# Two-layer graph network on one Trainium2 core: layer one's first score stage moved behind the plain block, weight and token sums dealt out by a kept clock per engine, token sums in a lent tile place

## Chip, cores and metric

The kernel runs on one core of one Trainium2 chip. The metric is the device time in microseconds (us) of that core, as the median of several runs. The kernel before takes 2650.01 us (three runs, 2649.26 to 2651.77).

## What is computed

The input x has 128 graphs of 64 nodes with 768 features, and adj is a 0/1 matrix of 64 by 64 for each graph. First h = relu(layernorm(x)). Then two layers follow, with weights of 768 by 768 each:

```python
m_left  = h @ W_left[l].T ;  m_right = h @ W_right[l].T
u_left  = h @ m_left^T / sqrt(768) ;  u_right = h @ m_right^T / sqrt(768)
u   = u_left on and above the diagonal of adj, u_right below it
att = exp(u)*adj / (row sum of exp(u)*adj + 1e-10)
ctx = att @ (h @ W_lin[l].T + b_lin[l])
h   = relu(layernorm(ctx, std with ddof=1, eps 1e-3) * a + b)
```

The result is x + h. Everything is in 32-bit floats. The weights are handed in transposed, and adj comes with its transpose beside it.

## The kernel before, in words

The 8192 tokens are cut into 32 parts of 256 tokens. A part's h lies transposed (features on the partitions) in an `ht` tile of six 128 x 256 chunks; six such tile places exist. The parts are grouped in blocks: block 0 has parts 0 and 1, blocks 1 to 10 have three parts each.

Each layer has two passes (the four calls stand at L1332 to L1335). **Pass one** makes M, the products of h with W_left and W_right combined, then the scores (L733, small matmuls of M with h), and from them the attention of a block (a chain of steps on POOL, DVE and ACT, `chain`, L737 to L779), which is stored to DRAM. **Pass two** multiplies with W_lin and applies the attention (L1006 and further).

In pass one a block of three parts is not multiplied plainly. A fast matrix multiplication scheme is used with 40 **products** (`PRODUCTS`, numbered 0 to 39). A product multiplies one sum of weight blocks, called a form (v = 18 to 118), with one sum of token blocks (T9 to T46), in eight matmuls of 128 x 256 at L702. Its result in a PSUM bank is read (L910 by ACT if it is the first into that part of M, L245 and L914 by DVE otherwise) and added into M. There are four banks in turn in a chain of products (C, D, X, Y, then C again), so product i+4 needs the reads of product i to be over.

- **Token sums** (`Tokens`, L583 to L638): 38 operations per block, on POOL, at L245, from `ht` chunks or earlier sums. `step` (L610) emits the next if the block's tokens are ready, if fewer than 11 (`LIMIT`) sums are out and if a buffer is free; `need` (L635) emits all that are missing right before the product that wants them. A token sum's buffer is a 128 x 512 place `g` of a common first-in-first-out list `free`; it goes back to the list when its last product is issued.
- **Weight sums** (`Weights`, L478 to L546): 101 operations, for layer one made on the chip while it runs, on DVE and POOL. `some` (L531) emits the first operation within reach whose operands exist. During the plain block an operand is first copied into a spare PSUM bank by ACT (L517; banks Z, V and the score bank in turn, `stage`), so that DVE reads only one operand from SBUF. For layer two the forms are made in pass two of layer one (`sums_ahead`, L549) and loaded from DRAM.

**What sets the order.** TensorE's program is written as a chain of products. Everything else is handed out in `turn_of` (L832), which is called twice for each product: once in its middle and once after it. Each call is a *slot*; product i of a block covers the slots 2i and 2i+1 after the block's first slot. `turn_of` runs what a plan has for that slot (`put`, `put_all`), then lets weight sums and one token sum follow as a small planner clock allows: `clock["vector"]` and `clock["pool"]` are compared with `now`, the estimated time of the slot. In the kernel before, this `clock` is a fresh local of each pass one (L830), starting at 0. Each engine carries out its own instructions in the order in which they were handed out.

**Layer one's block 0** is the *plain block*: 12 groups of 24 matmuls (L877 to L891), 72 slots, with no scheme, since the weight sums do not exist yet. Block 1 of layer one then begins with the scheme; in the kernel before the scores of block 0 come after its product 3 (`SCORED`, L925), the reads of products 0 to 3 behind the scores, and the attention chain at slot 2*SCORED+4 of block 1. Rows of x for the next parts are loaded, normalised (`mean_var` L333, L397 to L412), transposed (L465) and stored as h beside this (`prepare`, L850).

**The last block of pass one** (block 10) also gets `final` (L1310 to L1326): the W_lin blocks are loaded and centred on ACT (L233, L237), and from them come the sums N0 to N16 for pass two: Nn is planned at slot 42 + 3n//2 of the block, even n on POOL and odd n on DVE. The token sums for pass two's first parts (ta, u1, u2, u0, u3, td and more, on POOL) are planned at slots 56, 58 and so on.

Of the kernel before, what the change touches and what calls it, by code (L numbers as in the profile page):

```python
# [10 lines left out]
F32 = mybir.dt.float32  # L11
# [6 lines left out]
def kernel(  # L18
# [57 lines left out]

    def timed(us, f):
        f.vector = us
        return f

    def run(slot):
# [304 lines left out]
    def transpose_rows(l, u, pool):  # L386

        key, xr, todo = (1, l, u), XR[l, u], []
        if l == 0:
            mv = stat.tile([P, Q, 2], F32, name="mv0", bufs=2)  # L390
            sd = stat.tile([P, Q], F32, name="sd0", bufs=2)
            rs = stat.tile([P, Q], F32, name="rs0", bufs=2)
            nb = stat.tile([P, Q], F32, name="nb0", bufs=2)

            def scale(q0, q1):
                def deviation():
                    nc.scalar.activation(sd[:, q0:q1], mv[:, q0:q1, 1], AF.Sqrt, bias=eps_in)  # L397
# [16 lines left out]
            stats = [timed(1.2, lambda q=q: mean_var(mv[:, q, :], [xr[q][:, :HH], xr[q][:, HH:]])) for q in range(Q)]  # L414
            norms = [lambda q=q: norm(q) for q in range(Q)]
            if u:
                for f in stats + [lambda: [f() for f in scale(0, Q)]] + norms:
                    todo.extend([f, None])
            else:

                dev, inv = zip(*(scale(q, q + 1) for q in range(Q)))
                todo.extend([stats[START[0]], dev[START[0]]])
                for q, after in zip(START, START[1:] + (None,)):
                    if after is not None:
                        todo.append(stats[after])
                    todo.append(inv[q])
                    if after is not None:
                        todo.append(dev[after])
                    if q == START[2]:

                        todo.append(lambda: turn(0, START[0]))
                    todo.append(norms[q])
# [31 lines left out]
        for q in range(Q):  # L464
            todo.append(timed(0.9, lambda q=q: nc.vector.transpose(  # L465
                xb[:, :, q, :], xr[q].rearrange("p (b j) -> p b j", j=32))))
            todo.append(None)
# [3 lines left out]
    def places(pool, shapes, names):  # L471
        for n in names:
            shape, bufs = shapes[n]
            pool.tile(shape, F32, name=n, bufs=bufs)

    class Weights:  # L478
        def __init__(self, ops, plain, stay, extra=()):
# [10 lines left out]
            self.mine = {id(t) for t in extra}  # L490
            self.extra = deque(extra)

        def used(self, v):
# [5 lines left out]
        def take(self):  # L499
            of = max(self.extra, free, key=len)  # L500
            return of.popleft() if of else None

        def emit(self, eng, op):
            v, a, ca, b, cb = op
            x, y = self.at[a], self.at[b]
            dead = next((s for s in (a, b) if self.uses[s] == 1 and not (self.mine and s >= 18)), None)
            t = self.take() if dead is None else self.at[dead]
            if t is None:
                return False
            if dead is not None:  # L510
                self.uses[dead] = 0
                del self.at[dead]
            if self.stage and eng is nc.vector:
                bank = self.stage.pop(0)
                self.stage.append(bank)
                bank = bank.rearrange("p (c d) -> p c d", c=K2)
                nc.scalar.copy(bank, x)  # L517
                x = bank
            if ca == 1:
# [10 lines left out]

        def some(self, eng, reach=10):  # L531
            for op in self.left[:reach]:
                if op[1] in self.at and op[3] in self.at and (eng is nc.vector or op[2] == 1):
                    if eng is nc.vector and op[2] == 1 and any(o[2] != 1 and o[1] in self.at and o[3] in self.at
                                                               for o in self.left[:reach // 2]):
                        continue
                    return self.emit(eng, op)
            return False

        def need(self, v):  # L540
            if v not in self.at:
                op = next(o for o in self.left if o[0] == v)
                self.need(op[1])
                self.need(op[3])
                assert self.emit(nc.vector, op)
            return self.at[v]  # L546

# [35 lines left out]
    class Tokens:  # L583
        LIMIT = 11

        def __init__(self, l):
# [5 lines left out]
            self.count = {}  # L592


        def value(self, k, v, cut=False):
# [14 lines left out]
        def step(self, slot, eng=None):  # L610
            if self.k >= len(SUPER) or slot < self.ready.get(self.k, 10 ** 9) or self.out >= self.LIMIT or not free:
                return False
# [26 lines left out]


    SPACE = (((0, 46, 97), (-12, 34, 97)), ((10, 46, 97), (10, 46, 97)))

# [12 lines left out]
    def pass_one(l, start, final):  # L655
        with tc.tile_pool(name=f"one{l}", bufs=2, reuse_waits="tile") as sp, \
# [172 lines left out]
            weights.at = W[l, "raw"]  # L829
            clock = {"pool": 0.0, "vector": 0.0}  # L830

            def turn_of(slot):  # L832
                now = slot * 0.86 if l == 0 or slot >= 80 else slot * 0.6 + 20.8
                clock["vector"] = max(clock["vector"], now - 1.0) + sum(getattr(f, "vector", 0.0) for f in plan.get(slot, ()))
# [12 lines left out]

            follow = {}

            def prepare(b, slot, step=1):  # L850
# [5 lines left out]
                for t in range(2):  # L856
# [5 lines left out]
                    if before >= 0:  # L862
                        at = max(at, begins(where[before][0] + 1, l) + 2 * SCORED + 3)
                    put(at, lambda p=p, hold=before >= 0: load_part(1, l, p, hold))
                    put_all(at + lag + 6 * t, affine_part(1, l, p))
# [13 lines left out]
            for n, (w, t) in enumerate(order):  # L879
                bank = bank_of(n % CHAINS)  # L880
                for j in range(3):
                    tok = HT[1, l, t][:, j * K2:(j + 1) * K2, :]
                    product(bank, weights.at[3 * w + j], [tok], j == 0, slot)
                    weights.used(3 * w + j)
                    if j == 2:
                        if n == 0 and mid:
                            mid()
                            weights.stage = [KEEP["Z"], KEEP["V"], KEEP["scores"][:, 0]]
                        nc.scalar.copy(into(6 * t + w), out_of(bank))
                    turn_of(slot + 1)  # L890
                    slot += 2  # L891
            weights.stage = []

            last = len(SUPER) - 1
            for k in range(FIRST_OF[l], len(SUPER)):
                assert slot == begins(k, l)
                if k:
                    put_all(slot + 2 * SCORED + 4, softmax(k - 1), 3)
                    put(slot + 2 * SCORED + 42, lambda k=k: load_adj(k, nc.scalar))
# [4 lines left out]
                def reads(i):  # L904
                    for o, c in READS[i]:
                        bank = out_of(bank_of(CHAINS * (k - 1) + i % CHAINS), k == 0, o)
                        to = into(o, k == 0)
                        if o not in seen:
                            seen.add(o)
# [6 lines left out]
                for i, (f, t) in enumerate(PRODUCTS):  # L916
# [448 lines left out]
```

## Time and profile before

| what | value |
|---|---|
| median of three runs | 2650.01 us (2649.26 to 2651.77) |
| the profiled execution | 2648.42 us, its span 2646.6 us |
| granted TensorE clock, mean | 0.995 |
| DVE busy | 1780.6 us (67%), 2888 instructions |
| ACT busy | 935.4 us (35%), 1969 instructions |
| POOL busy | 1763.1 us (67%), 1392 instructions |

All rows below are from that one profiled execution. Times count from the start of its span. A row of the timeline gives start, length, engine, source line, operation, result and operands, shape and the number of instructions of the same kind in a row (x24), and in brackets the idle time of the engine ahead of it and the instruction that ended it. Engines: PE is TensorE, DVE is VectorE, ACT is ScalarE, POOL is GpSimd, SP is the queue that issues DMAs.

### The profile page before, as it was taken

Reading aid. Unit: us, or ns where it says so; the run is one execution under the profiler, and the core shown is the slowest. Engines: PE = TensorE matmul, PEld = TensorE weight load, DVE = VectorE, ACT = ScalarE, POOL = GpSimd, SP = SyncE. Lnnn points to the kernel's source line nnn. Section 1 sums busy time; section 2 is a strip of 40 time slices with the busy share of each in tenths; the row PEclk is TensorE's granted clock in tenths of the full one; section 3 lists DMA queues with packets and bytes.
Section 4 is the critical chain, followed back from the end, with each engine's and each line's share of the span. In section 5 each row is a group of like instructions: output and inputs, shape, how many; then the busy total and the mean of one; then the engine's idle time right before and its main releaser. Section 6 shows DMA issues by size and latency. Waiting matters only on the chain. (4 is left out here: it accounts for less than half of the span.)

```text
span 2646.6 us, 47202 instructions
## 1 busy us (share of the span) xinstructions
PE 2591.6 (98%) x18122; PEld 2217.1 (84%) x18122; DVE 1780.6 (67%) x2888; ACT 935.4 (35%) x1969; POOL 1763.1 (67%) x1392
## 2 busy tenths in 40 slices
PE   9899999999999999999999999999999989999998
PEld 8788888888888888888798888888888878887886
DVE  7878787777768445554456667677666676666667
ACT  5522223223113244454542222122222335555453
POOL 4766676666668657676276666667666657878786
PEclk9999999999999999999999999999999999999999
DMA  7443534343421354445794424253532215555655
GB/s 220 113 111 86 124 93 110 93 119 79 98 60 56 123 156 149 159 139 182 219 282 101 121 68 108 71 129 93 136 98 70 67 49 157 157 167 166 177 161 146
DMA packets 258465, 331.84 MB, mean 125 GB/s; under 512 B 56002, under 2 KB 190402, under 8 KB 258242
## 3 DMA queue, kind: packets, MB, share of 16 engines
q1 hardware_dynamic: 241442, 320.56, 44.3%
q10 hardware_dynamic: 16800, 8.26, 1.2%
q8 instruction: 145, 2.38, 0.4%
q14 instruction: 78, 0.64, 0.1%
HBM read 213.39 MB, written 115.34 MB: 124 GB/s over the span
## 5 line engine op out<-in xcount | busy, mean ns | idle before, releaser
L245 POOL TENSOR_TENSOR g<-ht 128x512 f32<-128x512 f32 (+1 forms) x620 | 785.9, 1279 | 420.8 <-PE Z L702 71.6
L245 POOL TENSOR_TENSOR g<-g,g 128x512 f32<-128x512 f32 (+1 forms) x310 | 397.9, 1291 | 136.7 <-PE C L702 22.0
L245 POOL TENSOR_TENSOR g<-ht,g 128x512 f32<-128x512 f32 (+1 forms) x272 | 346.1, 1282 | 164.8 <-PE Z L702 42.8
L702 PE MATMUL X<-g,g 128*128 128x256 f32 (+1 forms) x1080 | 252.9, 377 | 6.0 <-DVE m L914 6.0
L1006 PE MATMUL Z<-g,g 128*128 128x256 f32 x1024 | 244.1, 380 | 3.5 <-ACT hl L300 3.2
L702 PE MATMUL C<-g,g 128*128 128x256 f32 x1008 | 239.7, 381 | 4.9 <-POOL g L245 2.2
L702 PEld LDWEIGHTS X<-g,g 128*128 128x128 f32 x1080 | 203.0, 191 | 34.8 <-DVE m L914 6.8
L702 PE MATMUL Y<-g,g 128*128 128x256 f32 (+1 forms) x968 | 225.7, 376 | 3.8 <-POOL g L245 3.8
L1006 PEld LDWEIGHTS Z<-g,g 128*128 128x128 f32 x1024 | 191.6, 190 | 35.8 <-issue 4.1
L379 ACT ACTIVATE ht<-ht,b_col,a_col 128x256 f32<-128x256 f32 x384 | 196.1, 591 | 69.0 <-DMA ht<-h 53.8
L702 PEld LDWEIGHTS C<-g,g 128*128 128x128 f32 x1008 | 190.5, 190 | 32.9 <-POOL g L245 3.5
L702 PE MATMUL Z<-g,g 128*128 128x256 f32 (+1 forms) x936 | 217.0, 375 | 0.0
L702 PE MATMUL D<-g,g 128*128 128x256 f32 x880 | 209.8, 381 | 1.8 <-POOL g L245 1.8
L702 PEld LDWEIGHTS Y<-g,g 128*128 128x128 f32 x968 | 182.0, 190 | 27.8 <-POOL g L245 4.2
L702 PE MATMUL V<-g,g 128*128 128x256 f32 (+1 forms) x840 | 194.6, 375 | 3.1 <-POOL g L245 1.6
L702 PEld LDWEIGHTS Z<-g,g 128*128 128x128 f32 x936 | 174.5, 190 | 23.1
L702 PEld LDWEIGHTS D<-g,g 128*128 128x128 f32 x880 | 168.1, 191 | 25.7 <-POOL g L245 2.5
L1006 PE MATMUL X<-g,g 128*128 128x256 f32 x768 | 182.7, 379 | 0.0
L702 PEld LDWEIGHTS V<-g,g 128*128 128x128 f32 x840 | 157.6, 191 | 23.3 <-POOL g L245 1.7
L1206 POOL TENSOR_TENSOR z<-z,b 128x768 f32<-128x768 f32 x62 | 112.7, 1829 | 81.7 <-DVE z L1203 77.2
L245 DVE TENSOR_TENSOR m<-m,Y 128x512 f32<-128x512 f32 (+2 forms) x196 | 126.5, 667 | 58.4 <-ACT m L910 35.7
L245 DVE TENSOR_TENSOR m<-m,D 128x512 f32<-128x512 f32 x180 | 118.2, 677 | 70.0 <-ACT m L910 51.3
(222 smaller groups left out, 4612.0 us busy)
## 6 DMA issues: line engine op xcount, KB each, us to landing
ht<-h SPq DMA_DIRECT2D x126, 768.0 KB, 6.3
h<-xb SPq DMA_DIRECT2D x124, 384.0 KB, 6.6
z<-z SPq DMA_DIRECT2D x128, 192.0 KB, 3.1
x<-z SPq DMA_DIRECT2D x128, 192.0 KB, 5.4
xr<-in_x_dram SPq DMA_DIRECT2D x120, 192.0 KB, 3.8
out_dram<-xr SPq DMA_DIRECT2D x120, 192.0 KB, 2.7
x<-in_x_dram SPq DMA_DIRECT2D x112, 192.0 KB, 5.4
g<-form SPq DMA_DIRECT2D x40, 256.0 KB, 5.6
```

Source lines behind the costliest of these rows:

```text
L245: (eng.tensor_add if sign == "+" else eng.tensor_sub)(o, a, b)
L379: nc.scalar.activation(ht, ht, AF.Relu, bias=cols[1][:, c:c + 1], scale=cols[0][:, c:c + 1])
L702: nc.tensor.matmul(o, w[:, c, g * P:(g + 1) * P], t, start=(new and g == c == at == 0), stop=(c == K2 - 1), skip_group_check=True)
L1006: nc.tensor.matmul(p[:, n], b[t][:, c, r * P:(r + 1) * P], w[s][:, c, :], start=(i in FIRST and i not in PRELOAD and n == c == 0), stop=(c ...
L1206: nc.gpsimd.tensor_add(zs[k], zs[k], rows["b"])
```

## The change

1. **The scores of block 0** are issued right behind the plain block, ahead of product 0 of block 1. Its attention chain is planned from slot 2 of block 1, and the reads of block 1's products follow each product at once.
2. **The planner's clock** is made once for the whole kernel, with an entry for each of DVE, ACT and POOL. It is set at the start of layer one's pass one only (`if not l`). Each weight sum gets an estimated start (`begins`) from when its operands, its buffer, its engine and its stage bank are free; `some` takes the one that can start first and none that would start over 3 us ahead. Weight sums that are still missing at the end of the plain block are staged through banks Z and V in block 1.
3. **The lent place.** The `ht` tile place of part 5 is taken early, and its three 128 x 512 thirds serve as buffers for token sums of block 1 that are last used before product 20 (`SOON`). The load of part 5 itself moves to slot 113 (`back`), behind those of parts 6 and 7 in the SP queue.
4. The row statistics of parts 2 to 5 start at slots 19 and 31 instead of 16 and 30, and POOL may take weight sums from slot 0 instead of slot 8. Set beside each other in order, the two programs have the same instructions on TensorE; the new one has 11 fewer on DVE, 6 fewer on ACT and 10 more on POOL, as more of the weight sums go to POOL ahead of slot 60. Twenty of the weight sums are now emitted behind the plain block, between the products 0 and 20 of block 1; before, three were.

The core of the diff:

```diff
+    clock = {"vector": 0.0, "scalar": 0.0, "pool": 0.0}
...
     def load_part(which, l, p, hold=False):
-        ht = HT[which, l, p] = big.tile([P, C, TH], F32, name="ht", bufs=6)
+        if (which, l, p) not in HT:
+            HT[which, l, p] = big.tile([P, C, TH], F32, name="ht", bufs=6)
+        ht = HT[which, l, p]
...
+        def begins(self, eng, op):
+            dead = self.dead(op)
+            t = self.at[dead] if dead is not None else (self.extra or free or (None,))[0]
+            x, y = (self.made.get(s, 0) for s in (op[1], op[3]))
+            at = max(y, self.until.get(id(t), 0), clock[NAMES[eng]])
+            if self.stage and eng is nc.vector:
+                x = max(x, clock["scalar"], self.until.get(id(self.stage[0]), 0)) + 0.6
+            return max(x, at)
...
+        def some(self, eng, reach, now):
...
+            at, _, op = min(ops)
+            return at <= now + 3 and self.emit(eng, op)
...
         def emit(self, eng):
             v, a, b, sign = self.queue.pop(0)
-            t = free.popleft()
+            t = (self.own if self.own and self.last[v] < SOON else free).popleft()
...
             if v >= 9 and n == self.uses[v]:
-                free.append(self.at.pop((k, v)))
+                t = self.at.pop((k, v))
+                (self.own if id(t) in self.mine else free).append(t)
...
-            clock = {"pool": 0.0, "vector": 0.0}
+            if not l:
+                clock.update(vector=3.0, scalar=0.0, pool=3.0)
...
             def turn_of(slot):
-                now = slot * 0.86 if l == 0 or slot >= 80 else slot * 0.6 + 20.8
+                now = slot * 0.87 if l == 0 or slot >= 80 else slot * 0.6 + 20.8
...
+                for e in clock:
+                    clock[e] = max(clock[e], now - 0.5)
...
                 if weights.left and slot >= start["weights"]:
-                    while clock["vector"] <= now and weights.some(nc.vector):
-                        clock["vector"] += 0.62
-                    if clock["pool"] <= now and start["pool"] <= slot < start["tokens"]:
-                        if weights.some(nc.gpsimd, 40):
-                            clock["pool"] = max(clock["pool"], now) + 1.35
+                    while clock["vector"] <= now + (2 if slot > 2 * PLAIN else 0.5) and weights.some(nc.vector, 10, now):
+                        pass
+                    if slot < start["tokens"]:
+                        while clock["pool"] <= now + 0.5 and weights.some(nc.gpsimd, 40, now):
+                            pass
+                tokens.limit = Tokens.LIMIT - 2 * bool(weights.left)
                 if clock["pool"] <= now + 1.5 and tokens.step(slot):
                     clock["pool"] = max(clock["pool"], now) + 1.35
+            if l == 0:
+                for p in range(2, 6):
+                    HT[1, 0, p] = big.tile([P, C, TH], F32, name="ht", bufs=6)
+                tokens.own.extend(HT[1, 0, 5][:, j * K2:(j + 1) * K2, :] for j in range(3))
+                tokens.mine = {id(t) for t in tokens.own}
+
+                def back():
+                    assert len(tokens.own) == 3
+                    tokens.own.clear()
+                    load_part(1, 0, 5)
+
+                put(begins(1) + 2 * SOON + 1, back)
...
-            weights.stage = []
+            weights.stage = [] if l else [KEEP["Z"], KEEP["V"]]
+            if not l:
+                scores(0)
...
-                    put_all(slot + 2 * SCORED + 4, softmax(k - 1), 3)
+                    put_all(slot + (2 * SCORED + 4 if l or k > 1 else 2), softmax(k - 1), 3)
...
-                    if i == SCORED and k:
+                    if i == SCORED and l + k > 1:
                         scores(k - 1)
-                    if i >= SCORED or k == 0:
+                    if i >= SCORED or l + k < 2:
...
-    pass_one(0, {"weights": 0, "pool": 8, "tokens": 60, 1: 16, 2: 30}, final_of(0))
+    pass_one(0, {"weights": 0, "tokens": 60, 1: 19, 2: 31}, final_of(0))
```

More of the change, by code (lines that the diff above doesn't have):

```diff
@@ L474, in places @@
             pool.tile(shape, F32, name=n, bufs=bufs)
+    NAMES = {nc.vector: "vector", nc.gpsimd: "pool"}
     class Weights:
@@ L505, in emit @@
             x, y = self.at[a], self.at[b]
-            dead = next((s for s in (a, b) if self.uses[s] == 1 and not (self.mine and s >= 18)), None)
+            dead, at = self.dead(op), self.begins(eng, op)
+            if dead is None and len(free) <= self.spare:
+                return False
             t = self.take() if dead is None else self.at[dead]
@@ L529, in emit @@
             return True
[L531 to L538, printed above, removed]
+        def some(self, eng, reach, now):
+            ops = [(max(self.begins(eng, op), now) + (0.4 if eng is nc.vector and op[2] == 1 else 0), n, op)
+                   for n, op in enumerate(self.left[:reach])
+                   if op[1] in self.at and op[3] in self.at and (eng is nc.vector or op[2] == 1)
+                   and (len(free) > self.spare or self.dead(op) is not None)]
+            if not ops:
+                return False
+            at, _, op = min(ops)
+            return at <= now + 3 and self.emit(eng, op)
         def need(self, v):
@@ L592, in __init__ @@
             self.count = {}
+            first = {t: i for i, (_, t) in reversed(list(enumerate(PRODUCTS)))}
+            for v, a, b, _ in reversed(T_OPS):
+                for s in (a, b):
+                    first[s] = min(first.get(s, 99), first[v])
+            self.last = {v: max([i for i, (_, t) in enumerate(PRODUCTS) if t == v] +
+                                [first[o] for o, *ab, _ in T_OPS if v in ab]) for v, *_ in T_OPS}
+            self.own, self.mine, self.limit = deque(), set(), self.LIMIT
         def value(self, k, v, cut=False):
@@ L610, in step @@
         def step(self, slot, eng=None):
-            if self.k >= len(SUPER) or slot < self.ready.get(self.k, 10 ** 9) or self.out >= self.LIMIT or not free:
+            if self.k >= len(SUPER) or slot < self.ready.get(self.k, 10 ** 9) or self.out >= self.limit or not free:
                 return False
```

64 lines of the change are left out of this document (49 added, 15 removed).

## The prediction

> **What bounds the kernel now.** I read the page first, then the waits and the timeline of TensorE over layer one's start, then the same engine and POOL in the last block of each pass one. The page:
>
> ```profile
> span 2646.6 us, 47202 instructions
> PE 2591.6 (98%) x18122; PEld 2217.1 (84%) x18122; DVE 1780.6 (67%) x2888; ACT 935.4 (35%) x1969; POOL 1763.1 (67%) x1392
> ```
>
> TensorE is busy for 2591.6 of 2646.6 us, so at most 55 us are idle, and its own work is the same in the new program. What the change can do is to fill holes of TensorE or to open new ones. The timeline of TensorE at the hole in question, and a window over it:
>
> ```profile
> 69.55 5.34 PE L702 MATMUL Y<-ht,g 128*128 128x256 f32 x24
> 77.08 2.51 PE L702 MATMUL C<-g,g 128*128 128x256 f32 x8 [2.19 <-POOL g L245]
> 81.39 3.78 PE L702 MATMUL D<-g,g 128*128 128x256 f32 x8 [1.79 <-POOL g L245]
> 84.96 2.03 PE L702 MATMUL X<-g,g 128*128 128x256 f32 x8
> 90.80 2.57 PE L702 MATMUL Y<-g,g 128*128 128x256 f32 x8 [3.80 <-POOL g L245]
> 93.30 5.16 PE L733 MATMUL sc<-m,ht 128*32 128x95 f32 x192
> 99.49 1.97 PE L702 MATMUL C<-g,g 128*128 128x256 f32 x8 [1.04 <-ACT m L910]
> 101.30 1.89 PE L702 MATMUL D<-g,g 128*128 128x256 f32 x8
> ...
> 106.48 1.89 PE L702 MATMUL C<-g,g 128*128 128x256 f32 x8
> ...
> 128.92 1.89 PE L702 MATMUL D<-g,g 128*128 128x256 f32 x8
> ```
> ```profile
> 74.89:99.49 24.60, 15.78 (x225) 12.52 (x225) 20.55 (x35) 14.57 (x27) 18.94 (x16) 0.79 0.50 127
> 99.49:128.92 29.43, 29.43 (x136) 25.83 (x137) 23.68 (x44) 12.74 (x21) 21.27 (x18) 1.00 0.30 66
> ```
>
> The last plain group ends at 69.55 + 5.34 = 74.89. The four rows of 8 matmuls up to 90.80 are products 0 to 3 of block 1, then come the scores (L733), and 99.49 is product 4; 128.92 is product 21. Between 74.89 and 99.49 TensorE is busy for 15.78 of 24.60 us at a granted clock of 0.79 (the columns of a window are length, then busy time of PE, PEld, DVE, ACT, POOL, then the clock). From product 4 on it runs without a gap: (128.92 - 99.49) / 17 = 1.73 us per product. All three waits name POOL at L245, the token sums; these in turn wait for buffers that DVE's late weight sums hold:
>
> ```profile
> 83.09 2.51 POOL L245 TENSOR_TENSOR g<-ht 128x512 f32<-128x512 f32 x2 [1.75 <-DVE g L522]
> 88.13 2.61 POOL L245 TENSOR_TENSOR g<-ht,g 128x512 f32<-128x512 f32 x2 [2.53 <-DVE g L522]
> ...
> 108.51 1.28 POOL L245 TENSOR_TENSOR g<-g,g 128x512 f32<-128x512 f32 x1 [0.52 <-PE C L702]
> ```
>
> **Step 1: the hole in layer one (gain).** The change puts the scores where the first waits were, and they need no token sum. Another block's scores of the same size show the full-clock price:
>
> ```profile
> 1399.42 4.13 PE L733 MATMUL sc<-m,ht 128*32 128x95 f32 x192
> ```
>
> I let them start at 74.75 (as a product follows 0.16 us before the modelled end of the one before it) and take 4.13 plus 0.5 for the last copies of M by ACT: product 0 at 79.4, and without any wait product 4 at 79.4 + 4 x 1.73 = 86.3 instead of 99.49. That is **13.2 us** at best. Three things take some of it back.
>
> (a) *POOL.* In the order of the new program T16 goes to a third of the lent place that is freed by product 1, and product 3 wants it. Product 1 ends at 79.4 + 1.73 + 1.89 = 83.0; POOL started 0.14 us after such an end (106.48 + 1.89 = 108.37, row at 108.51), so T16 starts near 83.15, and POOL's queue is in order: T16 to T23 are eight sums of 1.27 (2.51 / 2 in the row at 83.09), ready at 83.15 + 10.2 = 93.3. Product 7 wants T23 and would start at 79.4 + 7 x 1.73 = 91.5. Cost 1.8, and 0.3 more for the same at products 9 and 11: **2.1 us**.
>
> (b) *DVE.* Twenty weight sums now lie between products 0 and 20. One staged sum, one statistics step, one mask step and one transpose:
>
> ```profile
> 89.10 0.68 DVE L245 TENSOR_TENSOR g<-sc,g 128x512 f32<-128x512 f32 x1
> 89.70 1.59 DVE L245 TENSOR_TENSOR g<-g,g 128x512 f32<-128x512 f32 x1
> 91.21 1.01 DVE L336 BATCH_NORM_STATS2 st<-x 128x6 f32<-128x384 f32 x2
> 92.25 0.21 DVE L337 BATCH_NORM_AGGREGATE mv<-st 128x2 f32<-128x12 f32 x1
> ```
>
> Staged sums follow each other at 0.60 (89.70 - 89.10), so 20 cost 12.0. The window 99.49:128.92 shows 23.7 us of DVE work beside products 4 to 20 (their reads, the attention chain, transposes); three of the four row statistics at 1.2 lay ahead of it and now come along, 3.7. Sum 39.4 us against 21 x 1.73 = 36.3 for products 0 to 20: 3.1 too much, part of which may trail behind product 20 in the four banks. The bounds are 0 and 3.1 plus a late start; by the order of the reads against the banks I take **2.1 us**. ACT's 20 copies of some 0.6 have cover (12.74 busy of 29.43).
>
> (c) *One buffer.* T37 now takes the place that T36 leaves after product 20, and product 21 wants it: 0.16 (overlap lost) + 0.14 + 1.27 + the start of the matmuls, **1.7 us**; 0 if that place is not the last one. The row 81.39 shows a price beyond: after a gap of 1.79 the eight matmuls took 3.78 in place of 1.89, while after the gap of 1.04 at 99.49 they took 1.97. My 1.7 lies between; I take no slow clock here and keep 1.9 us for the range. [...]
>
> Step 1: 13.2 - 2.1 - 2.1 - 1.7 = **7.3 us gained**, with 3 and 11 as ends (all three twice as dear; only (a) left). The load of part 5, and SP's queue with it, I cost at nothing:
>
> ```profile
> ht<-h SPq DMA_DIRECT2D x126, 768.0 KB, 6.3
> ```
>
> Part 5 opens block 2 at slot 152, 39 slots or 34 us behind slot 113; such a load lands in 6.3 us, and the stores of attention that now stand ahead of it in SP's queue are wanted by pass two only. If that cover were gone, block 2's first token sums and so its first product would wait for what is missing.
>
> **Step 2: layer two (loss).** The clock is set for layer one alone. At the end of layer one's pass one `clock["pool"]` stands near 870 x 0.87 = 757, and in layer two `now` starts at 20.8. The condition `clock["pool"] <= now + 1.5` then fails up to slot (757 - 1.5) / 0.87 = 868 of 880. So no token sum of layer two's blocks is given out ahead: each is emitted by `need`, right before its product. In blocks 0 to 9 that hardly matters: POOL's queue is in order and mostly waits for buffers that TensorE frees, and a sum emitted late in the program still starts when its buffer is free. The rows of POOL and TensorE from 1500 to 2060:
>
> ```profile
> L245 POOL TENSOR_TENSOR g<-ht 128x512 f32<-128x512 f32 x134 | 169.8, 1275 | 100.2 <-PE X L702 33.3 <-PE Z L702 30.1 <-PE C L702 27.7
> PE sc L733 <- issue: 2.8, 5, 0.9
> ```
>
> The first shows the waits for TensorE, the second that TensorE waited for no sum there. I take 0 for these blocks; the other end is a rival below. In the last block POOL also carries the even N sums, and these wait for ACT and DVE. Before, the token sums were handed out ahead of most of them; now T39 (wanted by product 23) stands behind N2, T41 (product 25) behind N4 and T44 (product 32, slot 64) behind all that is planned up to slot 63: N8, ta, N10, u1, N12, u2, u0, N14. TensorE and POOL there, before:
>
> ```profile
> 2121.62 1.89 PE L702 MATMUL Y<-g,g 128*128 128x256 f32 x8
> ...
> 2125.07 1.89 PE L702 MATMUL D<-g,g 128*128 128x256 f32 x8
> ...
> 2137.22 3.38 PE L702 MATMUL X<-g,g 128*128 128x256 f32 x8 [3.10 <-DVE m L914]
> ...
> 2142.17 1.89 PE L702 MATMUL C<-g,g 128*128 128x256 f32 x8
> ```
> ```profile
> 2121.96 1.27 POOL L245 TENSOR_TENSOR g<-g,g 128x512 f32<-128x512 f32 x1 [3.37 <-ACT g L968]
> ...
> 2127.81 1.27 POOL L245 TENSOR_TENSOR g<-g,g 128x512 f32<-128x512 f32 x1 [2.11 <-ACT g L237]
> ...
> 2139.64 1.28 POOL L245 TENSOR_TENSOR g<-g,g 128x512 f32<-128x512 f32 x1 [1.94 <-DVE g L245]
> 2140.88 1.73 POOL L245 TENSOR_TENSOR g<-ht 128x512 f32<-128x512 f32 x1
> ...
> 2146.70 1.72 POOL L245 TENSOR_TENSOR g<-g,g 128x512 f32<-128x512 f32 x1
> ```
>
> The products are 23, 25, 30 and 32; the sums are N2, N4, N10, u1 and N14. N2 starts at 2121.96 whatever is ahead, so T39 ends at 2121.96 + 2 x 1.27 = 2124.5: product 23 is 2.9 late. N4 starts at 2127.81, then T41 ends at 2130.4: product 25 is 5.3 late. Product 30 waited 3.10 for DVE before; that wait now lies inside the delay, and product 30 comes at 2130.4 + 5 x 1.73 = 2139.0, 1.8 late. N10 waits for DVE's N9, which stands behind the reads around product 30: 2139.64 + 1.8 = 2141.4. From N10's start to N14's end POOL took 2146.70 + 1.72 - 2139.64 = 8.8, and T44 adds 1.27: 2151.5. Product 32 is **9.3 us** late, after some 8 idle. Behind the gap of 3.10 eight matmuls took 3.38 in place of 1.89; the same here adds **1.5**. T45 and T46 follow within the products' pace. Nothing takes it back: the scores behind wait for reads that move along, and pass two keeps TensorE full:
>
> ```profile
> 2200.00:2600.00 400.00, 400.00 (x2081) 323.61 (x2080) 273.94 (x332) 207.73 (x442) 315.80 (x205) 1.00 0.57 163
> ```
>
> Step 2: **10.8 us lost**; the ends are 6.4 (N10 not late, each of the eight sums at 1.27, full clock) and 13.
>
> **Sum.** -7.3 + 10.8 = +3.5 us. Against its own time the profiled execution would go from 2648.42 to 2651.9. That execution lies 1.6 under the median of 2650.01, so on the median I forecast **2653.5**. Within 0.2%, 5.3 us to either side, is about what a measurement of this kernel can tell from no change: 2644.7 to 2655.3 is "same".
>
> **The rivals.**
> - *A: layer two's late handing out costs nothing*, if POOL's sums there run far enough ahead of TensorE or N10 isn't late. For it: no product waited for POOL from 1500 to 2060. Against it: N10's row waits 1.94 for DVE, and T44 is behind it. Time 2650.0 - 7.3 = 2642.7.
> - *B: layer one gives nearly all*, since the copies in PSUM and four banks take up DVE's surplus: 13.2 - 2.1 = 11, time 2650.0 - 11 + 10.8 = 2649.8.
> - *C: layer one gives little*, 3 us: DVE's surplus of 3.1 shows in full and more, with T37's gap at half clock. Time 2650.0 - 3 + 10.8 = 2657.8. In its extreme the change doesn't do what it says: the scores move, and products 0 to 3 wait for token sums as before.
> - *D: slower by waits in every block of layer two.* The place of such a sum as T37 is freed two products before the sum is wanted, and no run-ahead is left: 2 x 1.73 - 1.89 - 0.14 = 1.43 us for a sum of 1.27. If DVE beside them stretches POOL's sums to 1.7, as at 2140.88, each block loses 0.3 to 1.3 us; the point from which it decides is a sum of 1.43. Ten blocks: 3 to 13, time 2656.5 to 2666, say 2661. Against it: the mean of 1275 ns in the row above.
>
> **How the numbers follow.** Forecast 0.50, A 0.07, B 0.13, C 0.18, D 0.12. Faster by over 0.2%: A, 0.07. Within: B and 0.43 of the forecast's own 0.50, 0.56. Slower: C, D and 0.07 of the forecast's upper end, 0.37. The range leaves out A and the upper part of D, with a tail: 2645 to 2662.
>
> **What would show it.** In the new profile's timeline: the L733 row of 192 matmuls directly behind 74.9, product 4 near 88, product 21 near 121.6, with waits for POOL at products 3 to 7 and at 21. In layer two's last block, about 5 to 9 us earlier in absolute time than now: three waits of TensorE for POOL L245, at products 23, 25 and 32, the last near 8 us and followed by a row of some 3.4 us; none for POOL in the blocks before it. I am wrong if product 32 doesn't wait, if waits for POOL stand in the earlier blocks, or if product 21 of layer one is less than 3 or more than 11 us earlier than 128.92.

## The result

The changed kernel takes 2659.96 us (median of five runs, 2658.99 to 2662.02) against 2651.51 us of the kernel before beside it. The ratio is 1.0035, with a 95% interval of 1.002 to 1.0049: it is slower by 0.35%, some 9 us. The profiled execution took 2658.99 us with a span of 2657.2, which is 10.6 us more than the span of before. The page of the changed kernel has the same number of TensorE instructions and a busy time only 2.0 us longer, so most of the difference is time in which TensorE is idle:

```profile
span 2657.2 us, 47190 instructions
PE 2593.6 (98%) x18122; PEld 2215.3 (83%) x18122; DVE 1780.3 (67%) x2876; ACT 933.8 (35%) x1965; POOL 1777.3 (67%) x1404
```

**Layer one.** The timeline of TensorE at the place of the change, in the changed kernel (L760 are the products, L791 the scores):

```profile
70.87 5.34 PE L760 MATMUL Y<-ht,g 128*128 128x256 f32 x24
76.14 4.14 PE L791 MATMUL sc<-m,ht 128*32 128x95 f32 x192
80.21 1.99 PE L760 MATMUL C<-ht,g 128*128 128x256 f32 x8
...
91.80 1.99 PE L760 MATMUL X<-ht,g 128*128 128x256 f32 x8 [0.58 <-POOL ht L253]
94.37 1.99 PE L760 MATMUL Y<-ht,g 128*128 128x256 f32 x8 [0.58 <-POOL ht L253]
96.20 1.89 PE L760 MATMUL C<-g,g 128*128 128x256 f32 x8
...
103.57 1.99 PE L760 MATMUL C<-ht,g 128*128 128x256 f32 x8
106.35 1.97 PE L760 MATMUL D<-g,g 128*128 128x256 f32 x8 [0.79 <-DVE m L253]
111.20 3.39 PE L760 MATMUL X<-ht,g 128*128 128x256 f32 x8 [2.89 <-DVE g L566]
114.39 2.19 PE L760 MATMUL Y<-ht,g 128*128 128x256 f32 x8
116.42 1.89 PE L760 MATMUL C<-g,g 128*128 128x256 f32 x8
...
123.73 1.99 PE L760 MATMUL Y<-ht,g 128*128 128x256 f32 x8 [1.97 <-POOL ht L253]
125.57 1.89 PE L760 MATMUL C<-g,g 128*128 128x256 f32 x8
128.92 1.99 PE L760 MATMUL D<-g,g 128*128 128x256 f32 x8 [1.47 <-POOL g L253]
```

The scores stand directly behind the plain block, as planned, and the big holes of before (3.80, 2.19 and 1.79 us) are gone. Yet the last row is product 21, and it starts at 128.92, where it started before. (That it is so to the hundredth is chance: in the profiles of experiments 1 and 3 below, whose programs for layer one are the same, it starts at 128.71 and 129.19.) The whole lead has been given back in small waits: product 0 starts at 80.21, 21 products at 1.727, the pace of rows without a wait, would take it to 116.5, and 12.4 us are lost on the way. Read as differences between rows, products 0 to 8 lose 96.20 - 80.21 - 8 x 1.727 = 2.2, products 8 to 12 0.5, products 12 to 16 116.42 - 103.57 - 4 x 1.727 = 5.9, products 16 to 20 2.2 and product 21 1.6.

**Layer two.** In the last block of pass one, TensorE and POOL in the changed kernel:

```profile
2119.25 1.89 PE L760 MATMUL X<-g,g 128*128 128x256 f32 x8
2124.21 2.62 PE L760 MATMUL Y<-g,g 128*128 128x256 f32 x8 [3.07 <-POOL g L253]
...
2130.35 1.99 PE L760 MATMUL D<-g,g 128*128 128x256 f32 x8 [0.73 <-POOL g L253]
2133.66 1.99 PE L760 MATMUL X<-g,g 128*128 128x256 f32 x8 [1.32 <-POOL g L253]
...
2150.22 3.78 PE L760 MATMUL C<-g,g 128*128 128x256 f32 x8 [5.93 <-POOL g L253]
2153.79 3.06 PE L760 MATMUL D<-g,g 128*128 128x256 f32 x8
2156.69 1.89 PE L760 MATMUL X<-g,g 128*128 128x256 f32 x8
```
```profile
2121.66 2.49 POOL L253 TENSOR_TENSOR g<-g,g 128x512 f32<-128x512 f32 x2 [4.59 <-ACT g L1056]
...
2127.80 1.26 POOL L253 TENSOR_TENSOR g<-g,g 128x512 f32<-128x512 f32 x1 [2.42 <-ACT g L245]
...
2131.11 1.27 POOL L253 TENSOR_TENSOR g<-g,g 128x512 f32<-128x512 f32 x1 [0.82 <-DVE g L253]
...
2140.20 1.27 POOL L253 TENSOR_TENSOR g<-g,g 128x512 f32<-128x512 f32 x1 [1.94 <-DVE g L253]
...
2148.91 1.26 POOL L253 TENSOR_TENSOR g<-ht 128x512 f32<-128x512 f32 x1
```

The rows of TensorE are products 22, 23, 25, 26, 32, 33 and 34. Those of POOL are N2 with T39, N4, N6, N10, and at last T44, which ends at 2148.91 + 1.26 = 2150.17, 0.05 us ahead of product 32. Two rows of the kernel before are products 22 and 34 there:

```profile
2119.89 1.89 PE L702 MATMUL X<-g,g 128*128 128x256 f32 x8
...
2145.62 1.89 PE L702 MATMUL X<-g,g 128*128 128x256 f32 x8
```

From product 22 to 34 it was 2145.62 - 2119.89 = 25.73 us, and now it is 2156.69 - 2119.25 = 37.44: **11.7 us** are lost here. At product 22 the changed kernel is still 0.6 us ahead, so this one stretch makes up the whole difference of 10.6. Between 1420 and 2090 us no product waits for POOL; the waits of TensorE in that window:

```profile
PE sc L791 <- issue: 1.2, 4, 0.4
PE Z L760 <- issue: 0.2, 1, 0.2
```

(In layer two's first block, ahead of that window, one product waits 0.5 us for POOL; in the kernel before, one waited 1.6 us there.)

### The profile page after: what moved, and what is told of

It is laid out like the page before. It is cut to its first block, busy times and chain, and to the rows that moved or that the text cites. A ratio compares the mean times of both kernels' runs of the same rounds, so it can differ in the third digit from the quotient of the medians.

```text
span 2657.2 us, 47190 instructions
## 1 busy us (share of the span) xinstructions
PE 2593.6 (98%) x18122; PEld 2215.3 (83%) x18122; DVE 1780.3 (67%) x2876; ACT 933.8 (35%) x1965; POOL 1777.3 (67%) x1404
## 5 line engine op out<-in xcount | busy, mean ns | idle before, releaser
L760 PE MATMUL X<-g,g 128*128 128x256 f32 (+1 forms) x1056 | 245.9, 376 | 6.0 <-DVE m L1002 3.6
L760 PE MATMUL C<-g,g 128*128 128x256 f32 x1000 | 240.1, 383 | 7.7 <-POOL g L253 5.9
L760 PEld LDWEIGHTS X<-g,g 128*128 128x128 f32 x1056 | 197.0, 190 | 34.4 <-DVE m L1002 4.3
L760 PEld LDWEIGHTS C<-g,g 128*128 128x128 f32 x1000 | 191.0, 192 | 36.0 <-POOL g L253 7.3
L760 PE MATMUL Y<-g,g 128*128 128x256 f32 (+1 forms) x928 | 216.3, 376 | 3.1 <-POOL g L253 3.1
L760 PE MATMUL Z<-g,g 128*128 128x256 f32 (+1 forms) x936 | 217.4, 375 | 0.2 <-issue 0.2
L760 PE MATMUL D<-g,g 128*128 128x256 f32 x856 | 203.7, 381 | 3.0 <-POOL g L253 2.2
L760 PE MATMUL V<-g,g 128*128 128x256 f32 (+1 forms) x840 | 193.8, 374 | 3.2 <-DMA g<-form 2.7
L760 PEld LDWEIGHTS Y<-g,g 128*128 128x128 f32 x928 | 174.2, 190 | 26.3 <-POOL g L253 3.5
L760 PEld LDWEIGHTS Z<-g,g 128*128 128x128 f32 x936 | 174.6, 190 | 23.5 <-issue 0.6
L760 PEld LDWEIGHTS D<-g,g 128*128 128x128 f32 x856 | 163.1, 191 | 26.9 <-POOL g L253 3.2
L760 PEld LDWEIGHTS V<-g,g 128*128 128x128 f32 x840 | 156.7, 190 | 23.7 <-DVE m L253 3.0
L1094 PEld LDWEIGHTS X<-g,g 128*128 128x128 f32 x768 | 145.7, 190 | 21.5 <-issue 1.6
```

The lines of the kernel that those rows point to most:

```text
L760: nc.tensor.matmul(o, w[:, c, g * P:(g + 1) * P], t, start=(new and g == c == at == 0), stop=(c == K2 - 1), skip_group_check=True)
L1094: nc.tensor.matmul(p[:, n], b[t][:, c, r * P:(r + 1) * P], w[s][:, c, :], start=(i in FIRST and i not in PRELOAD and n == c == 0), stop=(c ...
```

## The experiments

The times of the kernel before differ by some us from one set of runs to the next (medians of 2650.2 to 2653.8), so each kernel is given as a ratio to the kernel before, run beside it on the same chip.

**1. The clock set for layer two.**

```diff
             if not l:
                 clock.update(vector=3.0, scalar=0.0, pool=3.0)
...
+            else:
+                clock.update(vector=0.0, scalar=0.0, pool=0.0)
```

> The changed kernel with one more line: the clock is set to 0 for layer two as well, so token sums are handed out ahead there again. Theory (all of layer two's loss is the order in POOL's queue in the last block, 11.7 us by the two traces): 2648 us, 11 to 12 under the changed kernel and level with the kernel before or 1 to 2 us under it, and no wait of TensorE for POOL in layer two's last block, but the old one of 3.1 us for DVE at product 30. Rival (the loss comes from the other places of the buffers in the free list, or from DVE's share of the sums): 2655 us or more, with waits for POOL still there.

Measured: 2649.62 us, ratio 0.9992 (0.9984 to 1.0001). The waits for POOL in layer two's last block are gone, and the old wait for DVE is back at product 30:

```profile
2136.77 1.99 PE L760 MATMUL X<-g,g 128*128 128x256 f32 x8 [3.09 <-DVE m L1004]
```

One line takes back the whole loss, 1.0035 to 0.9992, 0.43% or 11 us. What is left of the change is worth nothing that can be told from zero.

**2. The loss alone, in the kernel before.**

```diff
-            clock = {"pool": 0.0, "vector": 0.0}
+            clock = {"pool": 757.0 if l else 0.0, "vector": 0.0}
```

> The kernel before with one number changed: in layer two the clock of POOL starts at 757 instead of 0, which is where the kept clock stands. Theory: the loss of the changed kernel comes along whole without any of its other parts, 10 to 12 us, so 2662 us, with waits for POOL at the products 23, 25, 26 and 32 of the last block, the last one near 6 us with a half clock behind it. Rival (buffers): within 2 us of the kernel before.

Measured: 2662.63 us, ratio 1.0041 (1.0028 to 1.0054), 11 us more. The same waits appear at products 23 and 32:

```profile
2127.96 3.44 PE L702 MATMUL Y<-g,g 128*128 128x256 f32 x8 [3.05 <-POOL g L245]
...
2153.97 3.78 PE L702 MATMUL C<-g,g 128*128 128x256 f32 x8 [5.93 <-POOL g L245]
```

So neither the other buffer places nor the other share of the engines is needed: the order of handing out is enough.

**3. The clock set at the last block only.**

```diff
                 if k == last:
+                    if l:
+                        clock.update(vector=0.0, scalar=0.0, pool=0.0)
                     final(slot, tokens)
```

> The changed kernel with the clock set to 0 in layer two at the last block alone; blocks 0 to 9 stay on demand. Theory (only the last block pays for the late handing out, since POOL waits for buffers anyway in the others): the same time as with the clock set for all of layer two, within 2 us, 0.999 of the kernel before, no wait for POOL in layer two. Rival D of the prediction (sums without run-ahead cost 0.3 to 1.3 us in each block): 3 us or more above the kernel with the clock set for all of layer two.

Measured: 2649.62 us, ratio 0.9996 (0.9987 to 1.0005), level with the first experiment. Blocks 0 to 9 hand out on demand here and lose nothing that can be told from zero (the two ratios, 0.0004 apart, are each known to about 0.0009, or 2.4 us), and in the profile no product waits for POOL from 1420 us to the end of pass one. The loss is that of the last block, and the prediction's rival D falls.

**4. The move of the scores alone, in the kernel before.**

```diff
             weights.stage = []
+            if not l:
+                scores(0)
...
-                    if i == SCORED and k:
+                    if i == SCORED and l + k > 1:
                         scores(k - 1)
-                    if i >= SCORED or k == 0:
+                    if i >= SCORED or l + k < 2:
```

> The kernel before with the move of the scores alone: scores of block 0 directly behind the plain block, reads of block 1's products not put off; the old clocks, no stage behind the plain block, no lent place. Theory (the move fills the time in which the first token sums are late, and POOL then sets products 3 and 4): scores at 74.8, product 0 near 79.4, product 3 still near 90.8, product 21 at 122 to 125 instead of 128.9, total 4 to 7 us less than before, 2645 to 2647. Rival (POOL's late sums only come back behind the scores as waits of the same size): product 21 at 127 to 129, total within 2 us.

Measured: 2655.65 us, ratio 1.0011 (1.0002 to 1.002). Neither theory had this: the scores themselves wait.

```profile
89.84 6.79 PE L733 MATMUL sc<-m,ht 128*32 128x95 f32 x192 [14.43 <-DVE g L245]
```

The score bank is one of the three banks through which DVE's weight sums are staged, and DVE is full up to 89.7 us (busy for 14.45 of 15 us from 75 to 90, in this kernel and in the kernel before, where its last staged sum from that bank starts at 89.10). Moved alone, the scores stand in line behind DVE's staged sums, 14.43 us. In the changed kernel they don't wait: it leaves fewer sums on DVE, and its staging keeps off the score bank from plain group 10 on. Which of the two is needed was not run.

**5. The attention chain of block 0 later** (with the clock set for layer two, as all that follow).

```diff
-                    put_all(slot + (2 * SCORED + 4 if l or k > 1 else 2), softmax(k - 1), 3)
+                    put_all(slot + (2 * SCORED + 4 if l or k > 1 else 24), softmax(k - 1), 3)
```

> As the one with the clock set for layer two, and the attention chain of block 0 planned from slot 24 of block 1 instead of slot 2, so that its steps (about 7 us of DVE) stand behind more of the late weight sums. Theory (products 12 to 16 lose 6.0 us because late weight sums stand behind attention steps, statistics and transposes in DVE's queue): the wait of 2.9 us for DVE at product 14 and the slow matmuls behind it go or shrink to under 1, product 21 at 124 to 126 instead of 128.9, 3 to 5 us less than with the clock set alone. Rival (the late weight sums wait for ACT's copies or for operands from POOL, not for DVE): product 14 waits as long, same time within 1 us.

Measured: ratio 0.999 (0.9981 to 0.9999), level with experiment 1. Half of the theory holds: the wait at product 14 goes, the gain doesn't come. Product 19 waits 5.25 us in place of 3.65, and product 21 comes at 128.07 in place of 128.71:

```profile
106.26 1.89 PE L760 MATMUL X<-ht,g 128*128 128x256 f32 x8
...
120.31 3.78 PE L760 MATMUL Y<-ht,g 128*128 128x256 f32 x8 [5.25 <-POOL ht L253]
...
128.07 1.99 PE L760 MATMUL D<-g,g 128*128 128x256 f32 x8 [1.47 <-POOL g L253]
```

POOL in the same run says why:

```profile
117.63 1.27 POOL L253 TENSOR_TENSOR g<-ht,g 128x512 f32<-128x512 f32 x1 [6.81 <-DVE g L566]
```

The token sum that leads to product 19 waits 6.81 us for a buffer that a weight sum on DVE holds, and that weight sum stands behind the reads of products 15 and 16. TensorE, coming earlier, meets the same buffer.

**6. The lent place kept longer**, alone and with experiment 5.

```diff
-    SOON = 20
+    SOON = 22
```

> As the kernel with the clock set for layer two, and the lent place kept two products longer (token sums last used before product 22 may go there, part 5's load at slot 117). Theory (T37's wait of 1.5 us at product 21 comes from having only T36's place): that wait goes, and as three more buffers are to be had up to product 21, the wait for a token sum at product 19 shrinks too; product 21 at 124 to 127 instead of 128.7; total 1.5 to 5 us less. Rival (DVE is full there, 14.9 of 15 us from 105 to 120, so that another wait takes the place): product 21 within 1 us, same total.

> The later attention chain and the longer lent place together. Theory of the buffers: the wait of 5.25 us at product 19 is a token sum whose buffer is freed by a late weight sum, so with three more buffers it goes; product 21 at 119 to 123, total 5 to 9 us under the kernel with the clock set alone, 2641 to 2645. Rival (the work of DVE sets it): product 21 at 126 to 129.

Measured: 0.9971 (0.9959 to 0.9982) alone and 0.9969 (0.9959 to 0.998) with the later chain. The wait at product 21 goes in both. Alone, product 21 still comes at 128.00 and not at 124 to 127, since product 14 waits for DVE as before; yet the total is some 5.6 us under that of experiment 1, which neither theory had. Together, TensorE has only short waits left up to product 21 (the longest 1.47), and product 21, in the kernel of both, comes 9.0 us earlier than before:

```profile
119.93 1.90 PE L760 MATMUL D<-ht,g 128*128 128x256 f32 x8
```

This is the lead that the change was predicted to bring, 7.3 us, and more. In this profile it shrinks to 5.3 us at the next scores (163.39 against 168.73), mostly as products 30 and 31 wait for DVE's delayed steps (1.31 and 0.92 us at 137.83 and 140.75), then to 1.8 at 755 us (755.07 against 756.87) and 0.9 at the last scores of pass one (862.01 against 862.89). What takes the rest was not followed up.

**7. The rows of parts 6 and 7 prepared later** (with the longer lent place; then with the later chain too).

```diff
-    SPACE = (((0, 46, 97), (-12, 34, 97)), ((10, 46, 97), (10, 46, 97)))
+    SPACE = (((10, 46, 97), (-12, 34, 97)), ((10, 46, 97), (10, 46, 97)))
```

> The longer lent place, and the preparation of the rows of parts 6 and 7 (statistics and transposes, some 9 us of DVE) begun 10 slots later; attention chain as in the changed kernel. Theory of DVE's load: 3 to 6 us of it leave the stretch from 80 to 120, product 14 waits less, product 21 at 121 to 125; total 3 to 7 us under the kernel with the clock set alone. Rival (what is moved is missed at block 2, whose first token sums need parts 6 and 7): product 21 earlier, but a wait for POOL or DMA at the start of block 2 near 163 us, and the same total.

> All three: longer lent place, later preparation of parts 6 and 7, later attention chain. If DVE's order is what holds layer one back: product 21 at 117 to 121, 8 to 11 us earlier than before, and the total 2639 to 2643. If block 2 then waits for parts 6 and 7: 2646 or more.

Measured: 0.9989 (0.9979 to 0.9999) and 0.999 (0.9981 to 0.9999): some 5 us worse than without this edit (the intervals of the first pair overlap a little). Product 14 doesn't wait, but the work comes back. In the first kernel product 21 is at 123.21, inside the range expected, and the next scores are at 170.58, 1.9 us later than in the kernel before. In the kernel of all three, product 21 is at 119.34 and product 22 waits for a token sum.

```profile
124.71 1.99 PE L760 MATMUL X<-g,g 128*128 128x256 f32 x8 [3.47 <-POOL g L253]
```

Its next scores then are at 168.75, where they were before (168.73). I had named the token sums of block 2 as the place where this is paid; it is paid earlier, in block 1.

**8. The lent place kept longer still.** As experiment 6 with the later chain, and `SOON = 26`.

> The clock set for layer two, the later attention chain, and the lent place kept for sums last used before product 26 (part 5's load at slot 125 instead of 117). Theory of the buffers: the waits left at products 9 and 15 (1.1 and 1.5 us, a sum that takes the place freed by the product before) stay or shift, that at 23 goes; product 25 at 125 to 127; total within 2 us of the kernel with 22. Rival (part 5 then comes too late for block 2): waits for POOL near 155 to 165 us and 2 us or more above it.

Measured: 2640.73 us, ratio 0.9966 (0.9954 to 0.9978), the fastest kernel of the study, 9 us under the kernel before and some 18 under the changed one; its interval does not part it from `SOON = 22`. In its profile product 21 is at 122.78, 6.1 us earlier than before, and product 25 at 129.68, later than the 125 to 127 expected; three waits of 1.5 us (products 15, 19 and 20) are sums that take the place freed by the product just before, as T37 did.

What stays open: the timed gain of these last kernels, 8 to 9 us, is not to be found in layer one's pass one of their profiles. At the last scores of layer one's pass one they are 0.9 and 0.2 us ahead of the kernel before (862.01 and 862.69 against 862.89), and the whole span is 2646.1 with 22 and 2640.2 with 26 against 2646.6. The profiled execution of the kernel before, at 2648.42 us, was faster than all 24 runs of that kernel beside the one with 22 (2650.24 to 2659.66), so one profile against another can't carry a gain of this size. Nor do the lead at product 21 and the timed gain go together: with the longer place alone the lead is 0.9 us and the ratio 0.9971, with both edits 9.0 and 0.9969, with all three 9.6 and 0.999.

Part of the gain is TensorE's clock. The mean granted clock over the runs was 0.9950 for the kernel before and 0.9969 beside it with 22, and 0.9951 and 0.9973 with 26. As TensorE is busy for 98% of the span, that is, as an estimate, 5.0 and 5.8 us of the 8 and 9. The clock also differs between single profiles: its mean is 0.995 in that of the kernel before and 0.998 in the one with 26. The kernel before has it at half in layer two at 1351.6 and at 2136.7 us, 3.4 us long each, and at the second its product 30 takes 3.38 us behind a gap of 3.10; with 26 product 30 takes 1.99 behind the same gap. From the first product of layer two to its first scores it was 63.8 us before, 64.5 with 22 and 60.8 with 26. With one profile each, it can't be said how much of this is the kernel.

## Why the prediction was right or wrong

The forecast of 2653.5 was 6.5 us under the measured 2659.96, inside the range. Its likeliest case was no change; what came is slower by 0.35%, which it had given 0.37. The loss was right in its place, its cause and nearly its size. The gain was not: at product 21 there was none, so the result is the loss alone and not the small net of two terms that was forecast. The total is inside the range because the range was wide enough to hold rival C, not because the sum was right. By the prediction's own signs step 1 is wrong (product 21 was to come at least 3 us earlier) and step 2 is right (product 32 waits).

**Step 2, layer two: right.** Forecast 10.8, measured 11.7, and shown by experiments 1, 2 and 3 to be the clock that is kept and not set for layer two. The pieces: product 23 waits 3.07 (it was to be 2.9 late), product 32 is 8.7 us late counted from product 22 (9.3), and it starts as T44 ends, behind the sums that were named. Two things were missed. Product 26 waits 1.32 for T42 behind N6, which lies inside the later delay and leaves 5.93 of the 8 us of idle time forecast ahead of product 32. And the half clock behind the long gap covers two products, 3.78 and 3.06 us, so that it costs 3.0 and not 1.5; this makes up the difference. (The low end of 6.4 speaks of eight sums; from N10 to T44 there are seven, and 6.4 is worked out with seven.)

**Step 1, layer one: wrong in its size.** Forecast 7.3 gained at product 21, measured 0.0 (0.2 gained and 0.3 lost in the profiles of experiments 1 and 3). Term by term against the best case of 13.2: product 0 came at 80.21, not 79.4 (0.8; the plain block ends 1.3 us later, the scores are a bit faster). The late end is not the change's: the first plain group starts at 12.50 us in this profile and at 11.35 in that of experiment 1, whose program is the same up to there. (a) POOL's lent places, forecast 2.1, measured 2.2 up to product 8 and 0.5 more to product 12: right, and 0.6 too small. (c) T37 in T36's place, forecast 1.7, measured 1.6: right, and it brought no slow clock. **The step that failed is (b)**, DVE, forecast 2.1: products 12 to 16 lose 5.9, and product 19 another 2.2 through a buffer, 8.1 in all. The engine was named rightly, the way in which it costs was not. I set 39.4 us of DVE's work against 36.3 us of products as a whole and priced the surplus. There was no more work than that: DVE is busy for 37.6 us from product 0 to the end of product 20, and in the kernel of experiment 6 with the later chain TensorE gets from product 0 to product 21 in 40.8 us with DVE busy for 34.4 of them. What costs is the order in which DVE comes to it, and the buffers that are held meanwhile. The windows of the changed kernel show why a mean was too kind:

```profile
90.00:105.00 15.00, 13.65 (x61) 10.80 (x60) 11.01 (x22) 10.16 (x16) 12.39 (x11) 1.00 0.01 2
105.00:120.00 15.00, 11.32 (x44) 9.09 (x43) 14.93 (x29) 5.24 (x10) 4.43 (x4) 0.89 0.27 50
```

DVE (third busy column) has 4 us free from 90 to 105 and none from 105 to 120. And its queue is in order: the weight sum that product 14 waits for was staged in its bank by 105.1, but DVE came to it only behind these steps:

```profile
106.12 0.97 DVE L484 STREAM_TRANSPOSE xb<-x 128x768 f32<-128x768 f32 x1
...
108.33 0.97 DVE L484 STREAM_TRANSPOSE xb<-x 128x768 f32<-128x768 f32 x1
109.22 0.40 DVE L831 STREAM_TRANSPOSE wm<-adj 128x256 f32<-128x256 f32 x1
109.55 0.93 DVE L484 STREAM_TRANSPOSE xb<-x 128x768 f32<-128x768 f32 x1
110.41 0.65 DVE L566 SCALAR_TENSOR_TENSOR g<-Z,g 128x512 f32<-128x512 f32 x1
```

The order of DVE's program was known, so the term could have been worked out sum by sum against its product; whether that would have given 8.1 was not tried. Experiment 5 shows that it is the queue (the wait at 14 goes with the chain), experiment 6 that the wait at 19 was buffers.

**The rivals.** A (the late handing out costs nothing) and B (nearly all of the gain) did not come; D fell in experiment 3 and in the waits from 1420 to 2090 us. C, little gain in layer one, is what came: it said 3 us gained and 2657.8, and measured were 0 and 2660.0. It was right that DVE takes back far more than 2.1, though through its order and not through a surplus. The half clock that it put behind T37's gap did not come (1.99 us behind a gap of 1.47); one came at product 14 (3.39 behind 2.89). I had given C 0.18, too little beside the forecast's 0.50. That the scores alone would not do (experiment 4) was in none of the cases.

## What to carry to other kernels

A planner's state that outlives its use is part of a change: ask of every variable that becomes shared what it holds when the next phase begins. In queues that run in order, work handed out on demand cost nothing measurable here while the engine waited for buffers anyway, and 11 us in the one block where other work with waits of its own was handed out ahead of it. When a hole of one engine is filled, look for the engine that was busy in the hole: here DVE was nearly full from 60 to 90 us before (28.5 of 30 us) and full from 105 to 120 after (14.9 of 15), and its work, moved and not removed, made new waits. A lead at one product is not yet a gain in the total: kernels with leads of 0.9 and 9.0 us at product 21 took the same time.

## What the hardware showed

The same gap does not always bring the same clock. The wait of 2.89 us at product 14 was followed by eight matmuls of 3.39 us in the changed kernel and of 1.97 in the kernel with the clock set for layer two:

```profile
109.55 1.97 PE L760 MATMUL X<-ht,g 128*128 128x256 f32 x8 [2.89 <-DVE g L566]
```

The wait of 3.1 us at product 30 in layer two took 3.38 behind it in the kernel before, and 1.99 in that same kernel. With the lent place kept longer alone, a gap of 1.47, behind which product 21 of the changed kernel took 1.99, came 5 us behind a gap of 2.89, and the matmuls behind both were slow:

```profile
110.03 3.75 PE L760 MATMUL X<-ht,g 128*128 128x256 f32 x8 [2.89 <-DVE g L566]
115.25 3.78 PE L760 MATMUL Y<-ht,g 128*128 128x256 f32 x8 [1.47 <-POOL ht L253]
```

What stood ahead of a change of the clock can be read from the traces. In the profiles of the kernel before and of the changed kernel the times at which the granted clock changes lie whole multiples of 3.4133 us apart, to within 0.04 us, and so cut a profile into stretches. The gap of 2.89 us in the changed kernel, and then the same gap in the kernel with the clock set for layer two, laid over stretches of that length, in the second so placed that its slow row, 3.44 us at 122.07, fits them (the first busy column is TensorE's, the clock stands behind POOL's):

```profile
108.19:111.60 3.41, 0.52 (x3) 0.40 (x3) 3.41 (x7) 2.08 (x4) 0.00 (x0) 1.00 0.03 5
111.60:115.01 3.41, 3.41 (x10) 2.70 (x9) 3.41 (x7) 1.33 (x4) 0.27 (x1) 0.50 0.16 26
```
```profile
104.54:107.95 3.41, 2.12 (x10) 1.44 (x8) 3.34 (x9) 1.55 (x4) 0.72 (x1) 1.00 0.00 0
107.95:111.36 3.41, 1.81 (x9) 1.64 (x10) 3.41 (x7) 1.50 (x3) 0.00 (x0) 1.00 0.10 17
111.36:114.77 3.41, 3.41 (x17) 3.02 (x16) 3.41 (x6) 1.18 (x2) 2.52 (x2) 1.00 0.16 24
```

In the first the whole gap lies in one stretch, 2.89 us idle, and the clock of the next is 0.50. In the second it is split, 1.29 and 1.60 us, and the clock stays at 1.00. Over the profiles of the kernel before and of the changed kernel, between 10 and 2620 us and by the rows' modelled ends, all 7 stretches at full clock with 2.08 to 3.41 us idle were followed by half clock. Of the 23 with 1.0 to 1.92 us idle one was, by 1.59 us, in layer two's first block of the kernel before, and of the 1487 with less none. A stretch at half clock was followed by full clock in all 8 cases with at most 0.57 us idle, and by half clock again in the two with 0.88 and 1.79.

With the longer place alone the mean clock was 0.66 from 105 to 120 us; by the slow rows that is, as an estimate, 0.50 from 109.2 to 119.4, so the clock was half already when the gap of 1.47 came. The same holds for the row at 81.39 of the kernel before, which the prediction read as the price of a gap of 1.79: the clock there is half from 78.4 to 85.2 us, from before that gap on, and the idle time ahead of it was the gap of 2.19 at product 0.
